# A third decay tile in PSUM, paid for with one bank of the shared work and one bank of the state sums

## The chip, the cores and the metric

The kernel runs on one core of one Trainium2 chip. The metric is device time in microseconds (us). Three runs of the kernel before gave 2097.81, 2102.75 and 2104.69 us; their median, 2102.75 us, is the time before.

## The reference

The input `x` has two batches of 1024 positions and 256 channels; everything is fp32. Four layers follow one another.

- Layer 0 (a Mamba block): layer norm with a conditional scale and shift, a projection to 512 inner channels, a causal convolution over four positions, a SiLU, and then a selective scan with 16 states for each inner channel. Its result is gated with `silu(z)` and projected back.
- Layer 1: the same kind of scan twice, once forward and once over the flipped positions, both gated by one SiLU branch and added.
- Layer 2: linear attention with a softmax over head channels and positions.
- Layer 3: softmax attention with 16 heads.

What the change touches is the scan. For each channel d, state n and position t:

```
dA_t = exp(dt_t * A)                       # the decay
h_t  = dA_t * h_(t-1) + (dt_t * u_t) * B_t  # the state
y_t  = sum over n of h_t * C_t  +  u_t * D  # the state sum
```

There are six such scans over all (layer 0 and the two ways of layer 1, for two batches), each over 512 channels x 16 states x 1024 positions.

## The kernel before, in words

**Tiles of a scan.** A tile is 128 partitions (32 channels x 4 states) by 1024 positions. A scan has 64 tiles: 16 groups of 32 channels, and for each 4 steps k over the states. Two tiles (two groups of 32 channels, same k) form a pair; four pairs (k = 0 to 3) make one state sum of 64 channels, which is folded into one PSUM bank `ys_t`. All six scans give 384 tiles, 192 pairs and 48 state sums. `chain` (L1007) writes the order of all of it out by hand: the engines run each their own instructions in the order in which the code issues them.

**One tile on the engines.**
- ScalarE (ACT) makes the decay: `decay` (L944) writes `exp(A * dt)` into a PSUM tile `dA_t` of two banks (`wide`, L72, two buffers).
- GpSimd (POOL) makes the inputs: `inputs` (L950, instruction L952) writes `dt*u*B` into an SBUF tile `hb_t` (eight buffers).
- VectorE (DVE) runs the recurrence: `tile` (L955), instruction L963, or L959 for the reversed scans, as one scan instruction. It then multiplies with C into the `hb_t` tile (L966).
- For some even tiles, `far`, the scan writes to `hb_t` instead, and POOL does the multiplication with C (L965). A running balance `lead` decides which: it weighs DVE's work against the other work given to POOL.
- TensorE (PE) folds the 4 states of each channel together: `fold` (L984, L990) adds both tiles of a pair into the `ys_t` bank. `begin` (L968, L976 and L980) opens a new bank with `u*D`, and, for the second way of layer 1, the first way's result.
- `finish` (L995) takes the bank out: on DVE with the gate (L998) for scans 0, 1, 3 and 5, on ACT as a copy for scans 2 and 4. Two DMAs then save it.

**The order in a pair p.** First slot: inputs of tile 2p+3, decay of tile 2p+1, a slot of other work, tile 2p, decay of tile 2p+2, inputs of tile 2p+4. Second slot: other work, tile 2p+1, and at the end the fold of pair p-1. A state sum that ended with pair p-3 is taken out in pair p when k == 2, so three pairs after its last tiles:

```
ended = pairs[p - 3][:3] if p > 2 and k == 2 else None
```

**The other work.** `Behind` (L819) holds generators with everything that is not a scan: the projections, the norms and the inputs of the following scans. In each slot it takes steps from the first generator until the slot's credit of matmul columns (`RATES`, 1250 to 2048) or the room on ACT or POOL is used up. Nearly every step of it that has matmuls writes a PSUM bank `bank_t` (`bank`, L75) and has it read out by ACT (L133, L137) or DVE (L806 for the residuals, L1159, L1228, L1267 and L1286 in layer 2). There are two such banks. `pipe` (L375) and `projected` (L506) read a bank out one step after the last free one was filled, so with two banks the matmuls of one step run while the bank of the step before waits to be read. `ssm_inputs` (L569) holds two banks at a time for the two halves of `dt`.

**The PSUM pool of the scan stage** holds 8 banks of 512 columns: `dA_t` 2 x 2, `bank_t` 2, `ys_t` 2. The attention of layer 3 comes after the scans with a pool of its own (7 banks for scores, one for sums).

**DMA.** SyncE's queue (SP) issues all transfers: the spread rows of dt and dt*u (`sp`, L913), B and C rows (`bc`, L904), `fu` (L930), the gate `fg` (L941, one buffer, loaded in the pair with k == 3), and all saves.

Of the kernel before, what the change touches and what calls it, by code (L numbers as in the profile page):

```python
# [10 lines left out]
F32 = mybir.dt.float32  # L11
# [5 lines left out]
B, T, D, DI, N, R = 2, 1024, 256, 512, 16, 64  # L17
H, DH = 16, 16
P = 128
# [35 lines left out]
def kernel(ctx: ExitStack, tc: tile.TileContext, a: dict, out: bass.AP):  # L55
# [14 lines left out]
    psum = []  # L70

    def wide():  # L72
        return psum[-1].tile([P, T], F32, tag="dA", name="dA_t", bufs=2)

    def bank(tag=None):  # L75
        tag = tag or mode["bank"]
        return psum[-1].tile([P, 512], F32, tag=tag, name=f"{tag}_t", bufs=banks[tag])

    banks = {"bank": 2, "ys": 2, "av": 1, "sc": 7}


    mode = {"bank": "bank", "scans": False, "tail": False, "least": 640}
# [118 lines left out]
    sc = const.tile([P, 4, B], F32, tag="sc", name="sc")  # L201
# [367 lines left out]
    def ssm_inputs(key, u, w_xp, w_dt, dt_b, st):  # L569

        dbl = abuf((R + 2 * N, T))

        def low(ch):
            ps = bank()
            for k in range(4):
                mm(
                    ps[: R + 2 * N, :], w_xp[:, k, :], u[k][:, ts(ch, 512)],
                    start=(k == 0), stop=(k == 3),
                )
            return ps  # L580

        def take(ch, ps):
            act_copy(dbl[:, ts(ch, 512)], ps[: R + 2 * N, :])

        if key == "00":
            pss = [bank() for _ in range(2)]
            for k in range(4):
                for ch in range(2):
                    mm(
                        pss[ch][: R + 2 * N, :], w_xp[:, k, :], u[k][:, ts(ch, 512)],  # L590
                        start=(k == 0), stop=(k == 3),
                    )
            for ch in range(2):
                nc.vector.tensor_copy(dbl[:, ts(ch, 512)], pss[ch][: R + 2 * N, :])
        else:
            yield from pipe(*(
                (lambda ch=ch: low(ch), lambda ps, ch=ch: take(ch, ps)) for ch in range(2)
            ))
        st["bc"] = dbuf((2 * N, T), f"bc_{key}")
        save(2, st["bc"], dbl[R : R + 2 * N, :])  # L600
        if "first" in st:
            later(2, st["first"])


        st["dt"] = dbuf((2, DI, T), f"dt_{key}")

        def high(d, ch):
            held[0] += 1
            ps = bank()
            mm(ps, w_dt[:, ts(d, P)], dbl[:R, ts(ch, 512)], start=True, stop=True)  # L610
            return ps

        def parts(d, ch, ps, dt, dtu):
            held[0] -= 1
            act_f(dt[:, ts(ch, 512)], ps, AF.Abs, bias=col(dt_b, d))
            if key == "00" and d == 0:
                nc.vector.tensor_scalar(
                    dtu[:, ts(ch, 512)], ps, col(dt_b, d), 0.0, ALU.add, ALU.max
                )
            else:  # L620
                act_f(dtu[:, ts(ch, 512)], ps, AF.Relu, bias=col(dt_b, d))

        def both(d, o, x, y, op):

            if key == "00" and d == 0:
                nc.vector.tensor_tensor(o[:, :512], x[:, :512], y[:, :512], op)
                nc.gpsimd.tensor_tensor(o[:, 512:], x[:, 512:], y[:, 512:], op)
            else:
                far_op(o, x, y, op)

        two = banks["bank"] == 2
        pss = [high(0, ch) for ch in range(1 + two)]
        yield
        for d in range(4):
            dt, dtu = abuf(), abuf()
            parts(d, 0, pss[0], dt, dtu)
            if not two:
                pss.append(high(d, 1))
                yield
            parts(d, 1, pss[1], dt, dtu)  # L640
            yield
            act_f(dt, dt, AF.Exp, scale=-1.0)
            act_f(dt, dt, AF.Ln, bias=one)
            if d < 3:
                pss = [high(d + 1, ch) for ch in range(1 + two)]
            yield
            both(d, dt, dt, dtu, ALU.add)
            save(3, st["dt"][0, ts(d, P), :], dt)
            if key != "00":
                yield  # L650
            both(d, dtu, dt, u[d], ALU.mult)
            save(3, st["dt"][1, ts(d, P), :], dtu)
            later(3, lambda d=d: st["have"].append(d))
# [353 lines left out]
    def chain(scans, rates, early, mid, after):  # L1007

        pairs = [
            (i, d, cp, k)
            for i in range(len(scans)) for d in range(4) for cp in range(2) for k in range(NK)
        ]
        made = {"decay": {}, "inputs": {}}

        def ahead(n, kind):
            if n < 2 * len(pairs):
                i, d, cp, k = pairs[n // 2]
                made[kind][n] = getattr(scans[i], kind)(4 * d + 2 * cp + n % 2, k)  # L1020

        def fold(p):
            i, d, cp, k = pairs[p]
            if k == 0:
                scans[i].begin(d, cp)
            scans[i].fold(d, cp, k, [made["inputs"].pop(2 * p + j) for j in range(2)])

        def following(p):

            q = p - pairs[p][3] + NK  # L1030
            if q < len(pairs):
                i, d, cp, _ = pairs[q]
                return scans[i], 4 * d + 2 * cp

        s = scans[0]
        behind.until(lambda: s.st["have"])
        for c in range(2):
            for w in range(2):
                s.load_spread(c, w)
        s.load_bc(0, 1)  # L1040
        for k in range(1, NK):
            for w in range(2):
                s.load_bc(k, w)
        s.load_rest(0, 0)
        ahead(0, "decay")
        made["inputs"][0] = s.inputs(0, 0, nc.vector)
        ahead(1, "inputs")
        ahead(2, "inputs")
        mode["scans"] = True
        spent.update(ACT=0, POOL=0, DVE=0)  # L1050
        lead = 0
        for p, (i, d, cp, k) in enumerate(pairs):
            s = scans[i]
            nxt = following(p)
            final = d == 3 and cp == 1
            if d == 3 and cp == 0 and k == 0:
                early[i]()
            if final and k == 3:
                mid[i]()
            if k == 0 and nxt:  # L1060
                for w in range(2):
                    nxt[0].load_spread(nxt[1], w)
            if k == 1 and nxt:
                nxt[0].load_spread(nxt[1] + 1, 0)
            if final and i + 1 < len(scans):
                scans[i + 1].load_bc(k, 0)
            if k == 3 and nxt:
                nxt[0].load_rest(nxt[1] // 4, nxt[1] // 2 % 2)
            ahead(2 * p + 3, "inputs")
            ahead(2 * p + 1, "decay")  # L1070
            behind.slot(rates[i])

            ended = pairs[p - 3][:3] if p > 2 and k == 2 else None
            if ended and not scans[ended[0]].gate:
                scans[ended[0]].finish(*ended[1:])

            lead += 2 * (2200 + 1200 - 2300) + spent["DVE"] - behind.given["POOL"]
            spent["DVE"] = behind.given["POOL"] = 0
            far = lead >= LEAD
            if far:  # L1080
                lead -= 2300 + 1200
            lead = min(lead, 3 * 2300)
            rest = s.tile(
                4 * d + 2 * cp, k, made["decay"].pop(2 * p), made["inputs"][2 * p], far
            )
            if ended:
                if scans[ended[0]].gate:
                    scans[ended[0]].finish(*ended[1:])
                if ended[0] < i:
                    after[i - 1]()  # L1090
            if k == 3:
                s.load_gate(d, cp)
            ahead(2 * p + 2, "decay")
            ahead(2 * p + 4, "inputs")
            if rest:
                rest()
            if k == 1 and nxt:
                nxt[0].load_spread(nxt[1] + 1, 1)
            behind.slot(rates[i])
            s.tile(4 * d + 2 * cp + 1, k, made["decay"].pop(2 * p + 1), made["inputs"][2 * p + 1])  # L1100
            if final and i + 1 < len(scans):
                scans[i + 1].load_bc(k, 1)

            if p:
                fold(p - 1)
        fold(len(pairs) - 1)
        scans[-1].finish(3, 1)
        flush()
# [633 lines left out]
```

## Time and profile before

| what | value |
|---|---|
| median of three runs | 2102.75 us |
| span of the profiled execution | 2094.2 us |
| what lies around the span, median less span | 8.6 us |
| mean granted TensorE clock | 0.851 |
| first scan instruction on DVE starts | 64.5 us |
| last scan instruction on DVE ends | 1452.8 us |
| DVE busy over the span | 1748.3 us (83%) |
| POOL busy over the span | 1365.8 us (65%) |
| PE busy over the span | 1592.7 us (76%) |
| ACT busy over the span | 1140.8 us (54%) |

The profiled execution is told by its span alone; no other time of that one execution is given. The shares over the whole span mix three stages: the first 64.5 us until the scan starts, 1388 us of scans, and some 640 us of attention in which POOL does little. DVE's 384 scan instructions are 1388 us apart from first to last, 3.61 us for each. In that stage the long groups are POOL's inputs (383 of 2436 ns), DVE's scans (about 2285 ns each), DVE's product with C (285 of 1224 ns), POOL's product with C (99 of 2387 ns) and ACT's decay (384 of 1117 ns). A wait is listed with the engine that waits, the line it waits at, and the line that ended the wait.

### The profile page before, as it was taken

The numbers are of one execution on the slowest core, as the hardware profiler recorded it, in microseconds if no ns is written. First come the engines' busy times: TensorE is split into PE (matmuls) and PEld (weight loads), VectorE is DVE, ScalarE is ACT, GpSimd is POOL, SyncE is SP. The second block draws the span as 40 slices with busy tenths as digits, with TensorE's granted clock in tenths as the row PEclk, the third lists the DMA queues.
The fourth block names the chain that finished last, engine by engine and source line by source line (L and its number), as shares of the span: only waits on it lengthen the run. The fifth ranks groups of instructions, "written<-read, shape, count | busy, mean of one in ns | idle before, by whom it ended". The sixth has DMA issues, their size and how long they took to land. (4 is left out here: it accounts for less than half of the span.)

```text
span 2094.2 us, 22957 instructions
## 1 busy us (share of the span) xinstructions
PE 1592.7 (76%) x8112; PEld 605.6 (29%) x8112; DVE 1748.3 (83%) x1742; ACT 1140.8 (54%) x1592; POOL 1365.8 (65%) x666
## 2 busy tenths in 40 slices
PE   7576876389685637887955657834999999999997
PEld 3132213033141302222311333201544333333333
DVE  5798898898998999998998999998767657777763
ACT  4665775476546345664555455532154556656665
POOL 0799997998999999899998979997102111000000
PEclk9698988599797558988976978966899999999999
DMA  3673367264853555556763345343200111010001
GB/s 120 253 251 103 130 238 263 69 207 144 289 182 115 188 169 187 179 171 210 251 213 111 103 160 165 122 133 99 82 1 1 39 25 18 24 51 1 1 1 38
DMA packets 112503, 267.55 MB, mean 128 GB/s; under 512 B 16154, under 2 KB 40603, under 8 KB 112388
## 3 DMA queue, kind: packets, MB, share of 16 engines
q1 hardware_dynamic: 112388, 266.09, 38.2%
q8 instruction: 64, 1.05, 0.2%
q14 instruction: 51, 0.42, 0.1%
HBM read 195.91 MB, written 67.90 MB: 126 GB/s over the span
## 5 line engine op out<-in xcount | busy, mean ns | idle before, releaser
L952 POOL TENSOR_TENSOR hb_t<-sp,bc 128x1024 f32<-128x1024 f32 x383 | 918.7, 2436 | 62.9 <-PE ys_t L990 28.7
L133 ACT ACTIVATE dA_t<-sp,negA 128x1024 f32<-128x1024 f32 x384 | 428.3, 1117 | 530.4 <-DVE hb_t L966 446.4
L963 DVE TENSOR_TENSOR_SCAN dA_t<-dA_t,hb_t 128x1024 f32<-128x1024 f32 x195 | 445.8, 2286 | 43.8 <-ACT dA_t L133 29.0
L1442 DVE TENSOR_REDUCE mh<-sc_t 128x1 f32<-128x512 f32 x512 | 327.4, 684 | 114.2 <-PE sc_t L1433 110.6
L990 PE MATMUL ys_t<-hb_t,fold 128*32 128x512 f32 x1536 | 278.7, 735 | 167.2 <-POOL hb_t L965 110.5
L133 ACT ACTIVATE hb_t<-sc_t 128x512 f32<-128x512 f32 x512 | 276.7, 595 | 190.8 <-PE sc_t L1433 190.6
L966 DVE TENSOR_TENSOR hb_t<-dA_t,bc 128x1024 f32<-128x1024 f32 x285 | 349.0, 1224 | 22.1 <-DVE dA_t L959 0.5
L1433 PE MATMUL sc_t<-act_t 32*128 32x512 f32 x2048 | 337.3, 651 | 10.6 <-DVE mh L1442 8.8
L965 POOL TENSOR_TENSOR hb_t<-hb_t,bc 128x1024 f32<-128x1024 f32 x99 | 236.3, 2387 | 16.3 <-DVE hb_t L963 15.6
L799 POOL TENSOR_TENSOR act_t<-act_t,row 128x1024 f32<-128x1024 f32 x8 | 19.1, 2397 | 340.1 <-PE sc_t L99 191.9
L959 DVE TENSOR_TENSOR_SCAN dA_t<-dA_t,hb_t 128x1024 f32<-128x1024 f32 x90 | 205.7, 2285 | 11.8 <-POOL hb_t L952 7.4
L1473 PE MATMUL av_t<-hb_t,act_t 128*32 128x256 f32 x2048 | 164.7, 393 | 1.3 <-DVE act_t L1481 1.3
L95 PE MATMUL bank_t<-act_t,w_c_w 128*128 128x512 f32 x256 | 129.5, 656 | 37.0 <-ACT act_t L133 37.0
L133 ACT ACTIVATE act_t<-bank_t,cols 128x512 f32<-128x512 f32 (+1 forms) x206 | 129.6, 675 | 37.6 <-PE bank_t L95 29.5
L1433 PEld LDWEIGHTS sc_t<-act_t 32*128 32x128 f32 x2048 | 110.7, 186 | 121.4 <-issue 78.3
L990 PEld LDWEIGHTS ys_t<-hb_t,fold 128*32 128x32 f32 x1536 | 39.0, 119 | 362.7 <-POOL hb_t L965 149.5
L963 DVE TENSOR_TENSOR_SCAN hb_t<-dA_t,hb_t 128x1024 f32<-128x1024 f32 x61 | 139.0, 2278 | 4.3 <-ACT dA_t L133 3.9
L141 POOL TENSOR_TENSOR act_t<-act_t 128x1024 f32<-128x1024 f32 x50 | 119.2, 2384 | 0.2
L95 PE MATMUL bank_t<-act_t,w_dt_w 64*128 64x512 f32 x96 | 71.2, 876 | 43.9 <-ACT act_t L133 38.5
L99 PE MATMUL bank_t<-ident,act_t 128*128 128x128 f32 x128 | 34.3, 422 | 91.4 <-ACT act_t L133 91.2
L1473 PEld LDWEIGHTS av_t<-hb_t,act_t 128*32 128x32 f32 x2048 | 42.3, 108 | 191.5 <-issue 178.6
L1378 POOL MEMSET act_t<- 128x1024 f32 x8 | 7.6, 951 | 130.4 <-PE sc_t L1433 130.4
(178 smaller groups left out, 1811.6 us busy)
## 6 DMA issues: line engine op xcount, KB each, us to landing
sp<-dt SPq DMA_DIRECT2D x192, 512.0 KB, 5.5
bc<-bc SPq DMA_DIRECT2D x48, 512.0 KB, 6.8
dt<-act_t SPq DMA_DIRECT2D x48, 512.0 KB, 5.7
u<-act_t SPq DMA_DIRECT2D x24, 512.0 KB, 3.0
fu<-u SPq DMA_DIRECT2D x96, 128.0 KB, 3.4
y<-y SPq DMA_DIRECT2D x96, 128.0 KB, 3.6
g<-act_t SPq DMA_DIRECT2D x16, 512.0 KB, 5.4
fg<-g SPq DMA_DIRECT2D x64, 128.0 KB, 3.2
```

Source lines behind the costliest of these rows:

```text
L95: nc.tensor.matmul(o, w, x, **kw)
L133: nc.scalar.activation(o, x, func, **kw)
L141: nc.gpsimd.tensor_tensor(o, x, y, op)
L952: engine.tensor_tensor(e, self.sp[c, 1], self.bc[0][k], ALU.mult)
L959: nc.vector.tensor_tensor_scan(h[:, ::-1], dA[:, ::-1], e[:, ::-1], 0.0, ALU.mult, ALU.add)
L963: nc.vector.tensor_tensor_scan(h, dA, e, 0.0, ALU.mult, ALU.add)
L965: return lambda: nc.gpsimd.tensor_tensor(e, h, self.bc[1][k], ALU.mult)
L966: nc.vector.tensor_tensor(e, h, self.bc[1][k], ALU.mult)
L990: nc.tensor.matmul(self.ys[d, cp][at : at + DS, :], fold, e[:, ts(ch, 512)], start=False, stop=(k == NK - 1),)
L1433: nc.tensor.matmul(ps, w[r, ts(at, P)], x[r, ts(wide_at, 512)], start=True, stop=True)
L1442: nc.vector.tensor_reduce(mh[n][:, t, ch, j : j + 1], ps, AX.X, ALU.max)
L1473: nc.tensor.matmul(sums.av[32 * j : 32 * j + 32, ts(part, 256)], sts[b]["v"][t // 2][:, t % 2, 4 * g + j, :], es[j // 2][:, at : at + 256] ...
```

## The change

The 8 banks of the scan stage's PSUM pool are shared out anew: `dA_t` gets three buffers (6 banks), `bank_t` one bank, `ys_t` one bank.

- The decays are issued one tile earlier: in pair p the decays of tiles 2p+2 and 2p+3 in place of 2p+1 and 2p+2, and one more before the first pair.
- `finish` runs one pair sooner: two pairs after the last tiles of a state sum, at k == 1.
- `pipe` and `projected` are unchanged but read the number of banks, so they now read each bank out before the next step's matmuls.
- `ssm_inputs` takes its two halves of `dt` one after the other through the one bank, with one more step for each; before the scans start it uses `ys_t` as a second bank.

Lines from L631 on move up by one or two in the changed kernel: the scan L963 becomes L961, the product with C L966 becomes L964, `finish` L998 becomes L996, the fold L990 becomes L988, the residual L806 becomes L804.

```diff
-        return psum[-1].tile([P, T], F32, tag="dA", name="dA_t", bufs=2)
+        return psum[-1].tile([P, T], F32, tag="dA", name="dA_t", bufs=3)
...
-    banks = {"bank": 2, "ys": 2, "av": 1, "sc": 7}
+    banks = {"bank": 1, "ys": 1, "av": 1, "sc": 7}
...
-            pss = [bank() for _ in range(2)]
+            pss = [bank(tag) for tag in ("bank", "ys")]
...
-            ps = bank()
+            ps = bank("ys" if ch and not mode["scans"] else None)
             mm(ps, w_dt[:, ts(d, P)], dbl[:R, ts(ch, 512)], start=True, stop=True)
...
-        two = banks["bank"] == 2
-        pss = [high(0, ch) for ch in range(1 + two)]
+        ps = high(0, 0)
         yield
         for d in range(4):
             dt, dtu = abuf(), abuf()
-            parts(d, 0, pss[0], dt, dtu)
-            if not two:
-                pss.append(high(d, 1))
-                yield
-            parts(d, 1, pss[1], dt, dtu)
+            parts(d, 0, ps, dt, dtu)
+            ps = high(d, 1)
+            yield
+            parts(d, 1, ps, dt, dtu)
+            if d < 3:
+                ps = high(d + 1, 0)
             yield
             act_f(dt, dt, AF.Exp, scale=-1.0)
             act_f(dt, dt, AF.Ln, bias=one)
-            if d < 3:
-                pss = [high(d + 1, ch) for ch in range(1 + two)]
             yield
...
         ahead(0, "decay")
+        ahead(1, "decay")
...
             ahead(2 * p + 3, "inputs")
-            ahead(2 * p + 1, "decay")
+            ahead(2 * p + 2, "decay")
             behind.slot(rates[i])
 
-            ended = pairs[p - 3][:3] if p > 2 and k == 2 else None
+            ended = pairs[p - 2][:3] if p > 1 and k == 1 else None
...
-            ahead(2 * p + 2, "decay")
+            ahead(2 * p + 3, "decay")
             ahead(2 * p + 4, "inputs")
```

## The prediction, made before the changed kernel was run

> **What bounds the kernel now.** I read the page's busy shares and slices first, then the waits of DVE, POOL and ACT in the scan stage, then stretches of it, then the timeline at the places that the change moves.
>
> The slices show POOL and DVE at 8 or 9 tenths from slice 3 to 27 and PE alone at 9 behind: two stages with different limits. The change lies in the first.
>
> ```profile
> PE   7576876389685637887955657834999999999997
> DVE  5798898898998999998998999998767657777763
> ACT  4665775476546345664555455532154556656665
> POOL 0799997998999999899998979997102111000000
> ```
>
> The waits between 80 and 1475 us (engine, line, what ended it: us in total, times, longest), DVE's, POOL's and ACT's:
>
> ```profile
> DVE dA_t L963 <- ACT dA_t L133: 29.0, 18, 5.1
> DVE dA_t L963 <- POOL hb_t L952: 14.6, 15, 2.5
> ...
> DVE dA_t L959 <- POOL hb_t L952: 7.4, 5, 2.9
> ...
> DVE dA_t L959 <- ACT dA_t L133: 4.3, 3, 2.1
> DVE hb_t L963 <- ACT dA_t L133: 3.9, 1, 3.9
> DVE hb_t L959 <- ACT dA_t L133: 3.6, 3, 1.9
> ...
> POOL hb_t L952 <- PE ys_t L990: 28.7, 18, 4.0
> POOL hb_t L965 <- DVE hb_t L963: 15.6, 4, 7.2
> ...
> ACT dA_t L133 <- DVE hb_t L966: 444.8, 206, 13.2
> ```
>
> DVE waits 29.0 + 4.3 + 3.9 + 3.6 = 40.8 us for decays and 22.0 for POOL. ACT in its turn waits 445 us for DVE to release a decay tile: it has time, and is late only where other work stands between two decays.
>
> Where the waits lie (stretch; PE, PEld, DVE, ACT, POOL busy; clock, DMA):
>
> ```profile
> 108.00:285.00 177.00, 130.53 (x460) 48.81 (x459) 157.07 (x105) 118.05 (x152) 165.30 (x83) 0.87 0.47 159
> ...
> 1300.00:1455.00 155.00, 91.25 (x346) 25.62 (x344) 148.66 (x87) 67.06 (x75) 152.41 (x66) 0.75 0.36 113
> ```
>
> The first holds 16.6 us of waits for decays; in the second POOL is full and DVE waits for none. Here is one hand-over of a state sum:
>
> ```profile
> 220.10 8.82 PE L95 MATMUL bank_t<-act_t 128*128 128x512 f32 x16 [3.82 <-ACT act_t L137]
> ...
> 223.36 1.23 DVE L966 TENSOR_TENSOR hb_t<-dA_t,bc 128x1024 f32<-128x1024 f32 x1
> ...
> 225.52 0.69 ACT L133 ACTIVATE act_t<-bank_t,cols 128x512 f32<-128x512 f32 x1 [3.31 <-PE bank_t L95]
> ...
> 228.85 1.06 PE L990 MATMUL ys_t<-hb_t,fold 128*32 128x512 f32 x8
> 228.96 0.69 ACT L133 ACTIVATE act_t<-bank_t,cols 128x512 f32<-128x512 f32 x1 [1.74 <-PE bank_t L95]
> ...
> 229.84 1.07 PE L976 MATMUL ys_t<-fu,dgD 64*64 64x512 f32 x4
> ...
> 230.23 0.67 DVE L998 TENSOR_TENSOR y<-ys_t,fg 128x512 f32<-128x512 f32 x1
> ```
>
> PE ends the last fold of a sum at 229.9. DVE ended the product at 224.6 behind which the change puts L998. Where it stands now it waits for nothing; there it would have waited 5.3 us.
>
> **The change part by part.** Built, both programs have 4250 matmuls, 1590 ACT and 813 SP instructions; one product with C goes from DVE (285 to 284) to POOL (99 to 100).
>
> *Decays one tile earlier.* In pair p the decay of tile 2p+2 stands where that of 2p+1 stood. With three buffers it waits for tile 2p-1, exactly as that one did. ACT's own waits stay, and each decay is ready one tile (3.61 us) sooner. Of DVE's 25 waits only those of 5.1, 4.4 and 3.9 us exceed that, by 2.6 together: 38 us are there to gain if ACT keeps its place. In 108 to 285 it does not. There ACT follows PE (waits of 3.31 and 1.74 above): 8.82 us for two steps is 4.4 for one, and with one bank the readout of 0.69 no longer lies beside it, so each slot with such a step takes 5.1 against 3.61. I take 10 of the 16.6 us there and 22 of the rest: -32. Ends: 0 and -40.8. POOL permits it: its waits for a free input tile or a scan are 28.7 + 15.6 = 44 us.
>
> *State sums, one bank, taken out one pair sooner.* Of 47 hand-overs 31 are on DVE. I compared, from the timeline, the end of the last fold before each L976 with DVE's end of the first tile of the pair with k == 1. In 24 the fold is earlier, in 7 later, 15.2 us in all. If PE lagged 1 us more it would be 13 and 24.4 us, with 2 us more 17 and 40.0. With DVE faster and PE tied closer to ACT I take +20 (15 to 40). Queued behind L998 are all later scans. `begin` (L976) then waits for L998, 0.67 us after that product; it mostly starts 3 to 5 us after it as it is, held by other matmuls, so 0. Where PE was early, folds come some 4 us later, and with them the input tiles that they free; but POOL fills these for scans that are four tiles (14 us) off: 0, at worst 4 us where POOL stands at such a tile. The 16 hand-overs on ACT (0.58 us each) hold the next decay, which now has a tile to spare: 0, or the 4.9 us of late folds there if that is used up.
> The gate tile is loaded in the pair with k == 3. At the first change of scan its L941 is issued at 310.3 and lands at 318.0, 4.3 us after the new place; at the second it lands beside a fold that is 5.1 us late and counted. The others land 1.6 us or more ahead. +3 (0 to 5). The two saves of each sum go into SP's queue one pair sooner, and the loads of `sp` wait for decays that come earlier: nothing behind them on SP is held longer, 0.
>
> *One bank for other work.* On ACT, between two decays, there were 97 intervals with one readout of a bank, 51 with two, 13 with three; now 142, 38 and 7. Where there is one, the matmul was issued a slot before and is mostly done; its cover is ACT's 445 us of waiting. That cost is in the 10 of 16.6 above.
> DVE's readouts have no such cover. A residual step is 16 matmul records, 7.17 us for two, so 3.6; DVE adds in 0.69. With one bank the next 3.6 begin only after that, against a tile of 2.28 (far) or 3.5. The first residual has four readouts in consecutive slots: 3 x 1 us + 0.5. The other three groups are spread over more slots: 1 us each. In layer 2 the built order has two readouts L1159, two L1267 and three L1286 without a scan between: the second must wait for its matmuls, 1.8 (four records of 664 ns, overlapped), 2.1 + 1 for a fold, and 2 x 1.2; four L1228 some 0.5 each. Sum 3.5 + 3 + 1.8 + 3.1 + 2.4 + 2 = 15.8, so +15 (5 to 30: if half is hidden; if a fold stands before each).
>
> *Ahead of the scans.* The four groups of transposes take 3.97 us, 1.0 each, beside readouts of 0.8. In one bank they alternate: 3 x 0.9, and 0.4 for the bank's former use: about +3. The third wide tile lets PE start the third projection before DVE releases the first (its wait of 1.90 before 31.07, and DVE's gap of 1.27 there): -1. Together +2 (0 to 3.5).
>
> *One product on POOL:* +2.39 there, -1.22 on DVE: +1. *More steps in `ssm_inputs`:* in the new order the last readout of a bank comes some 16 tiles earlier than before, so nothing is left over for the attention: 0. Its stage of some 640 us uses other banks: 0.
>
> *Cover.* POOL-caused waits of DVE are 22 us. Some of the new waits fall into them: -4.
>
> Sum: -32 + 20 + 3 + 15 + 2 + 1 - 4 = +5. The execution's 2094.2 becomes 2099.2, and with the 8.6 us that lie around the span (median 2102.75) about 2107.8; I say 2107.
>
> A rule speaks against the change. The Trainium skill, "Perfetto Trace Analysis", section "Matmuls", has independent matmul groups rotate through different PSUM banks, so that readout overlaps the next group. The page's row of 206 readouts, 129.6 us, bounds what it could cost were PE the limit: 2107 plus up to 130, some 2240. PE is busy 0.74 of the first stretch above and 0.59 of the second, so I keep the sum without it.
>
> **The rivals.**
> - *Faster: the new waits hide.* DVE's new waits stand where it would otherwise wait for POOL, or PE keeps its lead. For it: 24 of 31 folds are early. Against it: the layer 2 readouts lie at 1110 to 1230, where by the timeline POOL ends an input 5 to 17 us before its scan starts. It gives -38 + 10 + 5 + 3 = -20: 2083.
> - *Slower: DVE runs ahead only to the next hand-over.* What a decay no longer stops, a fold does: it stands in PE's order behind matmuls that wait for ACT's readout, behind a decay. For it: at 220 to 230 ACT, PE and the fold are late together. It decides from about 1 us more lag of PE, where 13 of 31 are late; with 2 us the sum gains 20, to +25: 2127.
> - *The change does not do what it says:* ACT, tied to PE by one bank, uses up the spare tile and decays are late as before. For it: slots of 5.1 against 3.61. Against it: 445 us of ACT's waiting. Then the gain is 13 instead of 32: +24, 2126.
>
> **How the numbers follow.** The balance, 2107 with its own range of 2096 to 2118, has 0.38; the faster rival 0.27; the hand-over 0.23; the late decays 0.12. About 0.3% (6.3 us, so 2096.4 to 2109.1) is what a measurement here can tell from no change. Of the balance's 0.38, 0.22 lies within it, 0.14 above, 0.02 below; of the faster rival's, 0.02 within. Faster 0.27, same 0.24, slower 0.49. The range reaches to the faster rival and a little below, and past both slow ones: 2079 to 2136. The ends beyond (-40.8 with all new costs at their lowest; all at their highest) hold 2 in 10.
>
> **What would show it.** DVE's waits for decays fall from 40.8 us to under 12, most of what remains between 108 and 285. L998's successor waits for PE about 20 us in all, in some 10 places (now 2.0). DVE's waits for bank matmuls grow from about 10 to 25. The first scan starts at 66 to 67 us, not 64.5. POOL's waits for folds shrink. The attention's 640 us stay. I am wrong if hand-overs wait under 8 us (faster), or if decays or PE's folds fall behind over whole scans (slower).

## The result and the profile after

The changed kernel takes 2253.43 us (median of four runs, 2245.78 to 2266.81); the kernel before takes 2103.72 us beside it. The ratio is 1.073, 95% interval 1.069 to 1.076: the change costs 150 us. The prediction said 2107, at most 2136.

The profiled execution took 2259.7 us with a span of 2258.0: what lies around a span is 1.7 us, not the 8.6 us that I added (6.9 of those were the difference between two executions of the kernel before).

The first scan instruction starts at 65.7 us (before 64.5) and the last ends at 1613.8 us (before 1452.8); from there to the end it is 644 us (before 641). So nearly all the time is lost in the stage of the scans. Between its first and its last scan DVE is busy 1293 us (before 1282) and idle 255 (before 106). The slices of the page of the changed kernel, 56 us each, with the granted clock below:

```profile
PE   7476757378776638878755557854589999999997
...
DVE  5695687968889999999797667799777765777773
ACT  4654565454636446564544243443125455565665
POOL 0787688867989998999876556799600300100000
PEclk9687978689797559979677565876679999999999
```

POOL, which was at 9 tenths nearly throughout the stage, falls to between 6 and 8 in slices 1 to 9 (the first slice is slice 0) and to between 5 and 8 in slices 19 to 25, and DVE falls with it in most of them; in the second stretch layer 2 runs behind the scans. By the starts of the scan instructions, in blocks of 16 tiles, tiles 0 to 127 took 66 us longer, tiles 256 to 335 took 93 us longer, and the rest moved by less than 7 us a block. No engine has become full in these stretches. In 200 us of the second one (columns: window, length, busy us and instructions of PE, PEld, DVE, ACT, POOL, then granted clock, DMA share and GB/s):

```profile
1200.00:1400.00 200.00, 122.48 (x418) 54.61 (x416) 139.03 (x124) 73.52 (x101) 119.18 (x66) 0.64 0.29 96
```

PE is busy 0.61 of the stretch, DVE 0.70, POOL 0.60, ACT 0.37: they wait for one another. The waits of the changed kernel from 66 to 1640 us (engine, line, what ended it: us in total, times, longest):

```profile
ACT act_t L133 <- PE bank_t L95: 198.2, 100, 6.1
...
PE bank_t L95 <- ACT act_t L133: 181.4, 97, 16.6
POOL hb_t L950 <- PE ys_t L988: 158.6, 45, 14.6
...
DVE y L996 <- PE ys_t L988: 71.2, 15, 9.9
...
DVE act_t L804 <- PE bank_t L95: 39.6, 11, 11.9
DVE dA_t L961 <- ACT dA_t L133: 34.7, 13, 7.9
...
DVE qmx L1227 <- PE bank_t L95: 20.2, 4, 6.0
...
DVE y L996 <- DMA fg<-g: 19.0, 3, 7.8
```

And the same lines of the kernel before, in the same window:

```profile
PE bank_t L95 <- ACT act_t L133: 116.3, 46, 12.7
...
POOL hb_t L952 <- PE ys_t L990: 28.7, 18, 4.0
ACT act_t L133 <- PE bank_t L95: 27.9, 21, 3.5
...
DVE act_t L806 <- PE bank_t L95: 8.5, 4, 5.0
...
DVE y L998 <- PE ys_t L990: 2.0, 1, 2.0
```

ACT now waits 198 us for PE's matmuls before it can read the bank out, PE waits 181 us for ACT to have read it out (this row is the largest of several; with the rows of L99 and L137 it is 295 us, before 220), and POOL waits 159 us for folds that stand behind those matmuls in PE's order. DVE sets the end of the stage, so its waits have to add up to the loss, and nearly do:

| DVE's waits in the stage, us (rows of 1 us or more) | before | after | difference |
|---|---|---|---|
| for decays (four rows) | 40.8 | 49.4 | +8.6 |
| for the last fold of a state sum (L996) | 2.0 | 71.2 | +69.2 |
| for the gate tile (L996) | none | 19.0 | +19.0 |
| for matmuls of the shared bank (L804, L1158, L1227, L1266, L1285: 39.6 + 6.7 + 20.2 + 5.7 + 3.4) | 8.5 | 75.6 | +67.1 |
| for POOL's inputs (two rows) | 22.0 | 12.6 | -9.4 |
| sum | | | +154.5 |

This is the loop on the timeline of the changed kernel in layer 2 (start us, length, engine, instruction, and in brackets the idle time before it and what ended it):

```profile
1244.23 1.22 DVE L964 TENSOR_TENSOR hb_t<-dA_t,bc 128x1024 f32<-128x1024 f32 x1
...
1245.48 1.12 ACT L133 ACTIVATE dA_t<-sp,negA 128x1024 f32<-128x1024 f32 x1 [4.25 <-DVE hb_t L964]
1246.54 0.63 ACT L137 COPY act_t<-bank_t 128x256 f32<-128x256 f32 x2
...
1247.22 2.07 PE L95 MATMUL bank_t<-w_w,act_t 128*128 128x256 f32 x4 [3.71 <-ACT act_t L137]
...
1252.38 1.22 PE L95 MATMUL bank_t<-row,ones 1*128 1x256 f32 x2
...
1253.64 0.69 DVE L1227 TENSOR_REDUCE qmx<-bank_t 128x32 f32<-128x512 f32 x1 [5.99 <-PE bank_t L95]
...
1254.97 2.29 DVE L961 TENSOR_TENSOR_SCAN dA_t<-dA_t,hb_t 128x1024 f32<-128x1024 f32 x1
```

ACT waits 4.25 us for DVE's product, makes the decay that stands next in its order, and only then reads the bank out. PE has stood idle for 3.71 us and begins its step at 1247.2. DVE, which needs that step's result, waits 5.99 us for it. With two banks the same step of the kernel before, the second of four, began while the bank of the step before was still unread, and the reduction (L1228) found its result there without a wait:

```profile
1172.78 1.13 PE L95 MATMUL bank_t<-w_w,act_t 128*128 128x256 f32 x4
...
1173.77 0.63 ACT L137 COPY act_t<-bank_t 128x256 f32<-128x256 f32 x2
...
1175.53 0.69 PE L95 MATMUL bank_t<-row,ones 1*128 1x256 f32 x2
...
1179.17 0.66 DVE L1228 TENSOR_REDUCE qmx<-bank_t 128x32 f32<-128x512 f32 x1
```

The step took 3.44 us there and 6.38 us here. The pace alone does not make the wait: the first of the four steps (1232.14 to 1235.58) took 3.44 us in the changed kernel too, and DVE waited 4.82 us for it.

### The profile page after: what moved, and what is told of

It reads as the page before. It is cut to its first block, busy times and chain, and to the rows that moved or that the text cites. A ratio compares the mean times of both kernels' runs of the same rounds, so it can differ in the third digit from the quotient of the medians.

```text
span 2258.0 us, 22899 instructions
## 1 busy us (share of the span) xinstructions
PE 1667.6 (74%) x8112; PEld 617.4 (27%) x8112; DVE 1761.1 (78%) x1741; ACT 1141.8 (51%) x1592; POOL 1357.8 (60%) x667
## 5 line engine op out<-in xcount | busy, mean ns | idle before, releaser
L950 POOL TENSOR_TENSOR hb_t<-sp,bc 128x1024 f32<-128x1024 f32 x383 | 907.2, 2391 | 206.0 <-PE ys_t L988 158.6
L961 DVE TENSOR_TENSOR_SCAN dA_t<-dA_t,hb_t 128x1024 f32<-128x1024 f32 x194 | 443.3, 2285 | 40.5 <-ACT dA_t L133 34.7
L988 PE MATMUL ys_t<-hb_t,fold 128*32 128x512 f32 x1536 | 288.7, 794 | 140.6 <-POOL hb_t L963 92.2
L964 DVE TENSOR_TENSOR hb_t<-dA_t,bc 128x1024 f32<-128x1024 f32 x284 | 347.6, 1224 | 17.9 <-DMA bc<-bc 0.8
L963 POOL TENSOR_TENSOR hb_t<-hb_t,bc 128x1024 f32<-128x1024 f32 x100 | 236.2, 2362 | 19.1 <-DVE hb_t L961 19.0
L957 DVE TENSOR_TENSOR_SCAN dA_t<-dA_t,hb_t 128x1024 f32<-128x1024 f32 x90 | 205.6, 2284 | 13.0 <-POOL hb_t L950 6.9
L961 DVE TENSOR_TENSOR_SCAN hb_t<-dA_t,hb_t 128x1024 f32<-128x1024 f32 x62 | 141.4, 2280 | 4.2 <-ACT dA_t L133 4.0
L95 PE MATMUL bank_t<-act_t,w_c_w 128*128 128x512 f32 x256 | 124.4, 631 | 19.4 <-ACT act_t L133 19.4
L988 PEld LDWEIGHTS ys_t<-hb_t,fold 128*32 128x32 f32 x1536 | 38.9, 124 | 349.3 <-POOL hb_t L963 128.6
L974 PE MATMUL ys_t<-fu,dgD 64*64 64x512 f32 x192 | 74.9, 867 | 62.9 <-ACT y L137 33.8
L95 PE MATMUL bank_t<-act_t,w_xz_w 128*128 128x512 f32 x128 | 74.3, 709 | 30.0 <-ACT act_t L133 30.0
```

The source lines that it names most:

```text
L95: nc.tensor.matmul(o, w, x, **kw)
L950: engine.tensor_tensor(e, self.sp[c, 1], self.bc[0][k], ALU.mult)
L957: nc.vector.tensor_tensor_scan(h[:, ::-1], dA[:, ::-1], e[:, ::-1], 0.0, ALU.mult, ALU.add)
L961: nc.vector.tensor_tensor_scan(h, dA, e, 0.0, ALU.mult, ALU.add)
L963: return lambda: nc.gpsimd.tensor_tensor(e, h, self.bc[1][k], ALU.mult)
L964: nc.vector.tensor_tensor(e, h, self.bc[1][k], ALU.mult)
```

## The experiments

### Each part alone

**One shared bank alone.** Two decay tiles, decays and `finish` where they were, two state-sum banks; only the other work has one bank. Against the changed kernel:

```diff
-        return psum[-1].tile([P, T], F32, tag="dA", name="dA_t", bufs=3)
+        return psum[-1].tile([P, T], F32, tag="dA", name="dA_t", bufs=2)
...
-    banks = {"bank": 1, "ys": 1, "av": 1, "sc": 7}
+    banks = {"bank": 1, "ys": 2, "av": 1, "sc": 7}
...
```

> Two decay tiles, decays and state sums as before (two sum banks, taken out three pairs after), only the other work has one bank. Shared-bank theory (one bank ties PE to ACT step by step, and PE's folds and DVE's readouts fall behind it): most of the loss is here, 60 to 120 us over before, DVE's waits for decays clearly above 41 us, its waits for bank matmuls 40 us or more. Sum-bank theory (the loss is the hand-over of the one state-sum bank): DVE's readouts of the shared bank cost 30 to 50 us and little else, and L998's place waits for nothing.

Measured: 2249.12 us, ratio 1.069 (1.066 to 1.072), +145 us, more than the 60 to 120 that the shared-bank theory had. This part alone costs nearly all of the loss. Its waits:

```profile
PE bank_t L95 <- ACT act_t L133: 171.3, 97, 16.4
ACT act_t L133 <- PE bank_t L95: 158.9, 90, 4.5
...
DVE dA_t L961 <- ACT dA_t L133: 65.8, 34, 9.3
...
DVE hb_t L961 <- ACT dA_t L133: 38.7, 18, 6.0
DVE act_t L804 <- PE bank_t L95: 36.5, 11, 11.0
...
DVE dA_t L957 <- ACT dA_t L133: 21.1, 11, 4.4
DVE qmx L1226 <- PE bank_t L95: 20.9, 4, 6.0
```

DVE's waits for decays are 127.3 us with the row of 1.7 that is not shown (before 40.8), and those for the bank's matmuls 73.8 with three rows of 8.4, 4.6 and 3.4 (before 8.5): 86.5 + 65.3 = 152 us more. So one bank costs twice, each time through DVE: the decays come late because ACT waits for matmuls, and DVE's own readouts wait.

**One state-sum bank alone.** The kernel before with `"ys": 1` and `finish` one pair sooner.

```diff
-    banks = {"bank": 2, "ys": 2, "av": 1, "sc": 7}
+    banks = {"bank": 2, "ys": 1, "av": 1, "sc": 7}
...
-            ended = pairs[p - 3][:3] if p > 2 and k == 2 else None
+            ended = pairs[p - 2][:3] if p > 1 and k == 1 else None
```

> Two shared banks and two decay tiles as before; only the state sums have one bank and are taken out one pair sooner. Sum-bank theory: 60 to 100 us over before, DVE's waits at the taking-out near the 90 us (71 for folds, 19 for the gate tile) of the changed kernel. Shared-bank theory: the folds are late only because matmuls of the other work wait for the one bank; here the hand-over costs what I predicted for it, 15 to 25 us, and DVE waits there 20 to 30 us.

Measured: 2127.47 us, ratio 1.012 (1.009 to 1.015), +23 to +25 us. The waits at L998 are 16.7 us for folds in 7 places and 17.0 us for the gate tile in 3. PE, which opens the next sum in the same bank (`begin`, L976), waits 49.8 us for ACT's and 35.1 us for DVE's taking-out, neither of which it waited for before; the 23 us are what of all this reaches the end.

**Everything but the third tile.** The changed kernel with two decay tiles and the decays at their old places.

```diff
-        return psum[-1].tile([P, T], F32, tag="dA", name="dA_t", bufs=3)
+        return psum[-1].tile([P, T], F32, tag="dA", name="dA_t", bufs=2)
...
-        ahead(1, "decay")
...
-            ahead(2 * p + 2, "decay")
+            ahead(2 * p + 1, "decay")
...
-            ahead(2 * p + 3, "decay")
+            ahead(2 * p + 2, "decay")
```

> The changed kernel with two decay tiles, decays at their old place: everything that the change costs, without what it is for. If the third tile is worth what I predicted (32 us or more, more here as decays are late more often), it takes 2285 to 2330 us. If ACT, tied to PE, uses the spare tile up, it takes the changed kernel's 2253 within 10 us.

Measured: 2268.73 us, ratio 1.077 (1.073 to 1.081). This lies between the two expectations. The third tile is worth some 15 us in the company of the other two parts by the medians and 10 by the two ratios, whose intervals overlap, so its worth is small and not clear of the noise. It takes 71 us off DVE's waits for decays (120.1 here, 49.4 in the changed kernel), but the waits for folds at L996 rise from 26.2 to 71.2 us and those for the gate tile from 4.1 to 19.0. A DVE that no decay holds up arrives at the hand-over before PE does. The two costs nearly add up: 145 + 23 = 168 alone, 164 together.

### The physical bank, or the order that goes with it

**Two banks, in the order of one.** `pipe` and `projected` read each bank out before the next step, exactly as with one bank, so every engine has its instructions in the order of the run with one shared bank; but there are two banks, which the steps use in turn.

```diff
-    banks = {"bank": 1, "ys": 2, "av": 1, "sc": 7}
+    banks = {"bank": 2, "ys": 2, "av": 1, "sc": 7}
...
-            if len(waiting) == banks["bank"]:
+            if len(waiting) == 1:
...
```

> Each engine's instructions stand in the very order of the run with one shared bank (two decay tiles, two sum banks); only the matmuls of the other work alternate between two banks. If the loss is that PE may not start a step before the one bank is read out, it falls back to 2105 to 2150 us and PE's waits for ACT's readouts from 310 to under 220 us. If the loss is the order (each bank read out one step after its matmuls instead of two, so that ACT and DVE wait for PE), it stays at 2215 to 2250 us, with ACT's waits for bank matmuls still near 160 us.

Measured: 2121.89 us, ratio 1.009 (1.006 to 1.012), +19 us. From 1.069 to 1.009, 126 us, is the physical bank alone: with the second one PE may begin a step before the readout of the one before it, although ACT does that readout at the same place in its order. The waits, from an execution of 2108.66 us, the shortest of the five:

```profile
PE bank_t L95 <- ACT act_t L133: 104.6, 43, 18.0
...
ACT act_t L133 <- PE bank_t L95: 47.0, 31, 2.9
...
DVE dA_t L961 <- ACT dA_t L133: 24.1, 20, 4.8
DVE act_t L804 <- PE bank_t L95: 18.0, 7, 5.9
DVE hb_t L961 <- ACT dA_t L133: 16.9, 10, 7.8
```

ACT waits for matmuls 47 us instead of 159, DVE for decays 48 (with 7.3 at L957) instead of 127. The new order itself costs 19 us by the medians (13 to 25 by the interval).

**Three banks, in the order of two.** The run with one state-sum bank, every engine in that run's order, with the freed PSUM bank as a third for the other work.

```diff
-    banks = {"bank": 2, "ys": 1, "av": 1, "sc": 7}
+    banks = {"bank": 3, "ys": 1, "av": 1, "sc": 7}
...
-            if len(waiting) == banks["bank"]:
+            if len(waiting) == 2:
...
-        two = banks["bank"] == 2
+        two = True
```

> Edit: three banks for the other work instead of two, every engine's instructions in the order of the run with one state-sum bank and two banks for the other work (2127.47 us); only the physical bank that a step uses differs. Theory A (PE is still held by banks with two): another 5-15 us are won against 2127, and DVE's waits for the residual's bank fall from 22.5 us. Theory B (the second bank opens the loop, a third finds nothing to do): within 6 us of 2127.

Measured: 2121.18 us, ratio 1.009 (1.006 to 1.012), against 1.012 (1.009 to 1.015) for two banks. The difference of 6 us lies on the border between the two theories, and the intervals overlap: not decided. DVE's waits for the residual's bank fall from 22.5 to 17.0 us, as Theory A had it. What the run does show is that the step from one bank to two (126 us) is far larger than the step from two to three (6, and at the far ends of the two intervals 18).

### What the loop consists of

**The readout ahead of the decay.** In the changed kernel, each decay is issued after the slot's other work instead of before it. Shown for the first slot; the second is alike.

```diff
-            ahead(2 * p + 2, "decay")
             behind.slot(rates[i])
+            ahead(2 * p + 2, "decay")
...
```

> Edit: the changed kernel, with each decay issued after the other work of its slot and not ahead of it. With three tiles there is a tile of lead to give away. Theory A (the loss is a loop: ACT's readout of the one bank stands behind a decay that waits for DVE, PE may not begin the next step before that readout, and DVE later waits for PE): PE's waits for ACT's readouts of the bank, 181.4 + 50.0 us in the changed kernel, fall below 150 and the time falls to 2150-2210. Theory B (what costs is only that matmuls and readout of the one bank alternate, whatever stands between them): the time stays within 25 us of the changed kernel's 2253.

Measured: 2219.03 us, ratio 1.054 (1.050 to 1.059). That is 34 us better than the changed kernel (39 by the two ratios): more than Theory B allowed and less than Theory A wanted. PE's waits for ACT's readouts fall from 231.4 to 184.5 us (153.8 + 30.7), not below 150. The place shown above is mended: the four waits of the reduction L1227 fall from 20.2 to 4.6 us, and tiles 288 to 303 take 65.9 us instead of 90.7, most of the gain. But ACT's waits for matmuls stay (205.2 us, in the changed kernel 198.2), and DVE's for decays rise from 49.4 to 91.5: by the order, the decay now stands behind a readout that may have to wait for PE. So taking the decay from in front of the readout gives back some 34 us, after what the later decays cost. How the rest of the loss divides between these later decays and the bare alternation of matmuls and readout was not separated.

**The same in the kernel before.**

```diff
-            ahead(2 * p + 1, "decay")
             behind.slot(rates[i])
+            ahead(2 * p + 1, "decay")
...
```

> Edit: the kernel before, with each decay issued after the other work of its slot and not ahead of it. It has two banks and only one tile of lead. Theory A (with two banks the loop is open already): nothing is won, the decays come later, DVE's waits for them rise from 40.8 us to 60-100, and the time is 10-60 us above the kernel before. Theory B (the loop costs time in the kernel before too): 5-30 us are won.

Measured: 2108.29 us, ratio 1.0031 (1.0006 to 1.0057). DVE's waits for decays rise to 78.9 us as Theory A had it, but the time by 5 us only, less than its 10: other waits of DVE gave way. Theory B falls: with two banks the edit finds nothing to win.

**The fold ahead of the other work.** In the changed kernel the fold of pair p-1 is issued before the second slot's other work, so that no step stands in front of it.

```diff
+            if p:
+                fold(p - 1)
             behind.slot(rates[i])
...
-            if p:
-                fold(p - 1)
```

> The changed kernel with the fold of the pair before issued ahead of the second slot's other work, not behind it. If the loss comes through PE's order (folds held behind matmuls that wait for the one bank), DVE's waits at the taking-out fall from 71 to under 25 us and POOL's waits for folds from 159 to under 80 us: 2170 to 2210 us. If the loss comes through late decays and DVE's own readouts of the one bank, it stays within 25 us of 2253.

Measured: 2258.64 us, ratio 1.073 (1.070 to 1.076): nothing gained. The hand-over waits at L996 do fall, from 71.2 to 18.5 us, and POOL's for folds from 158.6 to 88.3. But DVE's waits for decays rise from 49.4 to 87.3, those at L804 to 43.3, and POOL's for DVE's scans (L963) from 19.0 to 68.7. A wait can be moved along the loop; its length stays here. The same edit in the kernel before:

> The kernel before with the fold of the pair before issued ahead of the second slot's other work. If folds held behind that work cost something with two banks, POOL's waits for folds fall from 29 to under 15 us and 5 to 15 us are won; if readouts are then late instead, it stays within 6 us of before or loses up to 10.

Measured: 2098.83 us, ratio 0.998 (0.996 to 1.000): the same time.

**PE kept busy.** The run with one shared bank, and in front of the matmuls of each step of other work four more matmuls that wait for nothing and that nobody reads.

```diff
+        if tag == "bank" and mode["scans"]:
...
+            for j in range(4):
+                nc.tensor.matmul(warm[0][:, ts(j, P)], ident, ident, start=True, stop=True)
```

> Edit: the run with one bank for the other work alone (2249.12 us); there PE has four more matmuls of 128 x 128 x 128 in front of the matmuls of each step of other work in the scan stage, into a PSUM bank of their own that nobody reads. They wait for nothing, so they fill time in which PE would wait for ACT to read the one bank out; their result is used by nobody. Theory A (PE's idling lowers the granted clock, 0.818 against 0.851 in the kernel before, and the slower matmuls are a good part of the 145 us): the clock rises by 0.02 or more, the real matmuls get shorter and the time falls by 15-60 us. Theory B (the loss is in the order of events, and the clock follows from it): the time stays or rises, by 0 to 60 us, since the extra matmuls (some 1.7 us in front of each step, by the 428 ns of a 128-column matmul in that run) also stand in the way where PE would not have waited.

Measured: 2250.47 us, ratio 1.071 (1.069 to 1.073), against 2249.12 without them. The granted clock rises from 0.818 to 0.877. Two of PE's groups in the run with one bank (after the first bar busy us and mean ns, then the idle time before them):

```profile
L95 PE MATMUL bank_t<-act_t,w_in_w 128*128 128x512 f32 x96 | 66.2, 826 | 40.6 <-ACT act_t L133 24.9 <-ACT act_t L137 15.7
L95 PE MATMUL bank_t<-w_w,act_t 128*128 128x256 f32 x96 | 40.0, 564 | 19.9 <-ACT act_t L137 13.9 <-ACT act_t L133 4.3 <-DVE act_t L804 1.6
```

And in this run, whose lines stand eight further down:

```profile
L82 PE MATMUL warm_t<-ident 128*128 128x128 f32 x1952 | 304.7, 305 | 0.0
...
L103 PE MATMUL bank_t<-act_t,w_in_w 128*128 128x512 f32 x96 | 50.8, 656 | 23.6 <-ACT act_t L141 13.9 <-ACT act_t L145 9.7
...
L103 PE MATMUL bank_t<-w_w,act_t 128*128 128x256 f32 x96 | 31.4, 463 | 9.5 <-ACT act_t L145 8.0 <-ACT act_t L141 1.4
```

Between 66 and 1640 us the real matmuls take 908 us (1212.4 less 304.7) instead of 1061.5, as many as there, and PE does 305 us of useless work; the time is the same. So giving the clock back in this way recovers nothing, and the lower clock looks like a companion of the loss; that the two effects, faster matmuls and more in front of them, happen to cancel is not excluded.

### Another place for the third tile

**Third decay tile in SBUF.** The kernel before with the decays one tile earlier and every third decay tile in SBUF (`dB_t`), so that the other work and the state sums keep two banks each. For its room the other work's tiles have one buffer less.

```diff
+    def wide(n=0):
+        if n % 3 == 2:
+            return third[0].tile([P, T], F32, tag="dB", name="dB_t", bufs=1)
         return psum[-1].tile([P, T], F32, tag="dA", name="dA_t", bufs=2)
...
-    act = ctx.enter_context(tc.tile_pool(name="act", bufs=15))
+    act = ctx.enter_context(tc.tile_pool(name="act", bufs=14))
...
```

> The kernel before with decays one tile earlier and a third decay tile in SBUF (every third tile), so that both shared banks and both sum banks stay; one buffer less for the other work's tiles. If my first term was right, DVE's waits for decays fall from 41 to under 10 us and 20 to 32 us are won: 2070 to 2085 us. If POOL or folds take the place of the decays, under 10 us are won. If scans or products with a decay in SBUF take longer on DVE or POOL, that shows in their mean durations, and it may be slower.

Measured: 2633.43 us, ratio 1.251 (1.248 to 1.255). DVE waits only 4.5 us for decays, as meant. But its scans with the decay in SBUF became slow. Two of DVE's groups (busy us and mean ns between the bars):

```profile
L967 DVE TENSOR_TENSOR_SCAN dB_t<-dB_t,hb_t 128x1024 f32<-128x1024 f32 x59 | 453.8, 7692 | 1.2 <-POOL hb_t L956 1.2
...
L967 DVE TENSOR_TENSOR_SCAN dA_t<-dA_t,hb_t 128x1024 f32<-128x1024 f32 x136 | 310.5, 2283 | 9.2 <-POOL hb_t L956 4.6 <-ACT dA_t L137 4.5
```

The view of the tile `dB_t` in that run has the least, median and most of those 59 durations in ns:

```profile
L967 DVE TENSOR_TENSOR_SCAN dB_t<-dB_t,hb_t x59: 2264/4439/22882, 71.8 to 1682.8; 128x1024 f32<-128x1024 f32 x59
```

The buffer that was taken from the other work, alone:

```diff
-    act = ctx.enter_context(tc.tile_pool(name="act", bufs=15))
+    act = ctx.enter_context(tc.tile_pool(name="act", bufs=14))
```

> Control for the run before: the kernel before with 14 instead of 15 tiles for the other work, nothing else. Expected within 10 us of before, 2095 to 2115 us; more would have to be taken off that run's difference.

Measured: 2110.13 us, ratio 1.0029 (1.0013 to 1.0046): 6 us of the 530.

None of the twelve kernels beats the kernel before.

## Why the prediction was wrong

**The step that failed is "One bank for other work".** I gave DVE's readouts +15, with 30 as the upper end, and ACT's side only the 6.6 us by which I cut a gain of 16.6 to 10, on the ground that "its cover is ACT's 445 us of waiting". Alone it costs 145 us, 126 of them the physical bank. Two mistakes made the number.

- *The cover was no cover.* ACT's 445 us of waiting for DVE stand in front of decays. ACT runs its instructions in order, so a readout that stands behind such a decay waits with it, as at 1245.48. With two banks PE could begin its next step meanwhile. With one, PE's next step hangs on that readout, ACT's next decay and DVE's readouts hang on that step, and DVE's progress releases the next decay: a closed loop in which each engine's waiting is a link and none of it is free. The runs show two pieces of it by themselves, the bank (126 us) and the decay in front of the readout (some 34 us); the loop as a whole is read from the waits and the timeline. I took the total of a wait and did not ask what stands behind it in the same queue when the readout becomes a condition.
- *I priced a step at the clock and the pace of the kernel before.* The step of layer 2 took 3.44 us there and 6.38 us here, and its matmuls went from 399 to 541 ns on average. The run in which PE is kept busy shortened the matmuls and won nothing, so this does not seem to be what holds the end; but a price built on the old durations was too low.

**The rule that I set aside was close.** The Trainium skill, "Perfetto Trace Analysis", section "Matmuls", has independent matmul groups rotate through different PSUM banks. From the row of 206 readouts (129.6 us) I worked out a bound of some 2240, 130 us of cost, and dropped it because PE was busy 0.74 and 0.59 of two stretches. The runs agree with the rule: going from two banks to one in the same order costs 126 us, and with the order that goes with it 145, more than my bound. PE was not the limit by its busy share, and the loop did not need it to be.

**The other terms.**

| term | predicted | in the changed kernel | alone or taken out |
|---|---|---|---|
| decays one tile earlier | -32 (0 to -40.8) | waits for decays +8.6 | third tile worth 10 to 15 beside the other parts, not clear of the noise |
| hand-over of the state sums | +20 (15 to 40) | +69 | 16.7 of waits alone |
| gate tile | +3 (0 to 5) | +19 | 17.0 of waits alone |
| DVE's readouts of the bank | +15 (5 to 30) | +67 | +65 in the run with one shared bank |
| cover by POOL | -4 | -9 | |

The two terms of the state sums together came out right alone, 23 predicted and 23 to 25 measured, but that is partly luck: the gate's part was far larger and the folds' smaller than I said, and the 20 for the folds had been raised for a DVE that runs faster, which that run does not have. The transfers of the gate are the part that I underrated: three of them, not one, came too late for the new place. With PE behind by the loop, the folds came later still, and the hand-over took most of what the third tile had given. I had put it at "from about 1 us more lag of PE"; PE lagged far more. I also put at 0 that PE has to wait with the next sum until the one bank is taken out. In the changed kernel this is 33.8 us behind ACT's copies and 10.1 behind DVE (L974), where the kernel before has no such wait:

```profile
PE ys_t L974 <- ACT y L137: 33.8, 6, 11.4
```

What that adds to DVE's waits was not separated.

**The rivals.** "DVE runs ahead only to the next hand-over" named the mechanism that the third tile's run shows (26 to 71 us of waiting for folds), and "late decays as before" the one that the run with one shared bank shows; but I priced them from single slots and hand-overs, as if each lateness ended where it arose, so 2127 and 2126 hold about a sixth of the loss. I wrote that I would be wrong if "decays or PE's folds fall behind over whole scans"; the folds did. The start of the scans (65.7 us, predicted 66 to 67) and the unchanged attention (644 us) came out nearly as said. POOL's waits for folds were to shrink; they went from 28.7 to 158.6.

## What to carry to other kernels

Before the number of buffers between two engines goes from two to one, follow the consumer's queue: if the readout stands behind an instruction that waits for a third engine, that engine's waiting is not cover but becomes part of the producer's wait. Here PE was busy 60 to 75% of the time, and the second bank was still worth 126 us of 2103; moving waits along the loop (fold first, decay later, a filled PE) gave back some 34 to 39 at most. A gain from running further ahead is worth only the distance to the next thing that the same engine will wait for: 71 us of decay waits removed were 10 to 15 us of time.

## What the runs showed of the hardware

A scan instruction on DVE with all operands in SBUF (`dB_t`) takes 2264 ns at best, like one that reads its decay from PSUM (2283 on average), but where it begins while POOL is at work it gives way: the 59 of the group above took 4.4 us in the median and up to 22.9. Of all 128 scans with their decay in SBUF, the 85 that took over 2.4 us all began while a POOL instruction ran; of the other 43, 39 began while POOL was idle. Here is one in the run with the third tile in SBUF, with DVE's and POOL's instructions around it:

```profile
502.86 2.41 POOL L956 TENSOR_TENSOR hb_t<-sp,bc 128x1024 f32<-128x1024 f32 x1
...
504.22 21.65 DVE L967 TENSOR_TENSOR_SCAN dB_t<-dB_t,hb_t 128x1024 f32<-128x1024 f32 x1
...
519.10 4.62 POOL L956 TENSOR_TENSOR hb_t<-sp,bc 128x1024 f32<-128x1024 f32 x2
525.91 1.22 DVE L970 TENSOR_TENSOR hb_t<-dB_t,bc 128x1024 f32<-128x1024 f32 x1
```

POOL works without a gap from 502.9 to 523.7 us, nine instructions, and the scan ends 2.2 us after the last of them: it made no progress that shows for as long as POOL had work. The Trainium skill, "SBUF — State Buffer", section "Who interferes with whom", says that a DVE instruction with two SBUF inputs contends with a GpSimd instruction that reads SBUF. The same section calls the pair of ports that the two share an exclusive lock. These rows agree with both, and go further: here the scan loses to a whole row of instructions and not to one. That is also what the decay in PSUM buys in this kernel.

The granted TensorE clock was 0.851 before, 0.818 with one bank, and 0.877 with one bank and 305 us of filler. The filler moved a matmul of 256 columns from 564 to 463 ns, and it did not move the time. PE's busy share alone does not tell the clock: between the first scan and the last it was 0.68 at a clock of 0.80 in the kernel before, and 0.71 at 0.78 with the fold ahead in that kernel.
